# A planned order of steps, replaced: a four-layer graph network whose instruction order is the result of annealing

## The chip, the core and the metric

The kernel runs on one core of a Trainium2 chip. A core has five engines with queues of their own: TensorE (PE, matrix products; PEld is its loading of weights), VectorE (DVE), ScalarE (ACT), GpSimd (POOL) and SyncE (SP), which here only issues transfers. Transfers run on 16 DMA engines that all queues share. The metric is the device time of one execution in microseconds (us); lower is better. The kernel before takes 2910.88 us (median of three runs, 2910.64 to 2910.99).

## The reference

There are 32 graphs (B) of 512 nodes (N) with 256 features (D) each, all in float32. Four layers follow each other; after each there is a residual addition and a normalisation over the features. Cut to what is computed:

```python
def _layernorm(x, axis=-1, eps=1e-5):
    m = jnp.mean(x, axis=axis, keepdims=True)
    v = jnp.var(x, axis=axis, keepdims=True)
    return (x - m) / jnp.sqrt(v + eps)
# layer 0: two-layer perceptron on aggregated neighbours
aggregated = jnp.einsum('bnm,bmd->bnd', adj, x)
h = (1.0 + eps) * x + aggregated
return jax.nn.relu(h @ W1 + b1) @ W2 + b2
# layer 1: four heads, additive scores, edges where adj > 0.5
e = jax.nn.leaky_relu(e_dst[:, :, :, None] + e_src[:, :, None, :], 0.2)
attn = jax.nn.softmax(jnp.where(mask, e, MASK_VAL), axis=-1)
out = jnp.einsum('bhij,bjhf->bihf', attn, h)          # + bias
# layer 2: eight heads, dot products, log of the adjacency added
scores = jnp.einsum('bhqd,bhkd->bhqk', q, k) / math.sqrt(HEAD_DIM)
attn = jax.nn.softmax(scores + jnp.log(adjacency + 1e-06)[:, None, :, :], axis=-1)
out = out.transpose(0, 2, 1, 3).reshape(b, n, HIDDEN) @ Wo.T + bo
# layer 3: scores through one matrix, times adj, nodes masked
similarities = jnp.einsum('bsd,btd->bst', matrix @ W, matrix) * adj
attn = jax.nn.softmax(jnp.where(key_mask, similarities, NEG_INF), axis=-1)
output = jnp.einsum('bst,bth->bsh', attn, matrix)
```

## The kernel before

The work is cut into some 370 small steps per graph, plus 71 that prepare the weights once (`prepare`, line 331, called graph 0). Each graph (`graph`, line 560 on) goes through the four layers, and steps of five to six graphs are in progress at once. A step has a name, an engine, a cost in us written in the code, the steps that it must follow, the buffers that it takes and frees, and for TensorE a mode. The instructions of a step are written out when the planner reaches it; the order in which it reaches them is the order of each engine's queue, since the kernel is recorded under a manual schedule (line 1458). So the order of everything, transfers included, is a product of the class `Plan` (line 47).

`Plan.order` (line 136) is a list scheduler. It keeps a clock for each engine. At each turn it looks at all ready steps of the graphs in its window, finds the earliest start, and takes, of those that can start within `ahead` of it, the one with the smallest due time. The due time of a step is

```python
due = turn[g] * period - self.left[g][name] + moved[name] + stay * change
```

`turn` is the graph's number (moved earlier for the last graphs by `rush`), `left` the longest chain of costs behind the step, `moved` an amount for each step name, and `change` what the planner believes a change of TensorE's mode costs, weighted by `stay`. `moved` is the sum of two things: the list of moves given for each name, and random disturbances that are replayed from seeds:

```python
for seed, far in shifts:
    rng = random.Random(seed)
    for n in moved:
        if rng.random() < 0.15:
            moved[n] += rng.uniform(-far, far)
```

`Plan.run` (line 217) plays each parameter set that it is given, keeps the best, and writes the instructions out; here one set is given. Since `moved` goes by name, every graph is treated alike, and in the middle of the run each graph's steps come in the same order.

The steps that matter below (k is a block of 128 keys of half of the heads, c a block of 128 nodes, the first digit of the names of layers 1 to 3 often the layer or head):

- Layer 0: `h0 h1` (line 728), `f0` to `f3` (751), `y0 y1` (770). `he`, `fe` are their evacuations by ScalarE. `at` (695) transposes the adjacency.
- Layer 1: `xt10 xt11` transpose x (798), `xe10 xe11` evacuate them and sum (802), `v10` to `v13` (819) are the values. `R` is an exponential of the scores; `Rt` transposes it (857), `Rsi` writes it to DRAM (867), `Rli` reads it back to all partitions (874). `z` (922, ScalarE) and `zm` (933, VectorE) make the weights of each head. `o100 o101 o110 o111` (956) multiply them with the values: first digit after o1 the pair of heads, second the half of the nodes. `as` (983, VectorE) adds each head's four blocks up, `d1` (993) sums over the partitions.
- Layer 2: `s0` to `s7` (1115) are four scores at once on 32 rows each, `e` their exponentials (1128, ScalarE), `m` the product with the adjacency (1137, VectorE), `n0` to `n7` (1173) the products with the values. `cd` and `fd` (1148, 1201) are transfers by POOL's queue that add one block of weights onto another, so that `d2` (1220) needs few matmuls. `xt20 xt21 q k v2` come before these, `p0 p1` (1299) after.
- Layer 3: `xt30 xt31`, `i0 i1` (1343), `t0` to `t3` (1357), `ta tb` (1373, 1379), `te` (1387), `u` (1396), `w` (1411).

On TensorE, `s` uses 32 rows of the array, `o1` 64 columns, `n` and `d1` 32 columns, `d2` 64 rows and 32 columns, and all other steps the whole array. The planner knows them as modes `row`, `c64` and `c32`. PSUM has 8 banks; each `s` step takes four of them, which its exponentials free.

Of the kernel before, what the change touches and what calls it, by code (L numbers as in the profile page):

```python
# [227 lines left out]
def fast_path(  # L228
# [71 lines left out]
    def blk(i):  # L300
# [3 lines left out]
    plan = Plan({  # L304
        "B": 11, "C": 12, "D": 18, "p": 8,

        "live": 6, "L0": 1, "L1": 2, "L2": 2, "L3": 1, "AT": 4, "zs": 7, "edge": 1, "tmp": 2,
    })
# [1147 lines left out]
    for g in range(B):  # L1456
        graph(g)
    with tc.manual_schedule():
        plan.run([(24, 0.1, 6, 165.0, ((959604, 5.0), (114893, 5.0), (451585, 5.0), (104136, 2.0), (561761, 2.0), (241046, 2.0), (593942, 2.0), (984585, 2.0)), (2.0, 1.1, 0.1), (('R', 0.5), ('Re', -5.0), ('Rl.q', 20.0), ('Rli', -15.0), ('Rs.q', 3.0), ('Rsi', 6.5), ('Rt', -62.0), ('ST', -37.5), ('ab', 6.0), ('as00', 6.5), ('as01', 6.0), ('as10', 0.5), ('as11', -1.0), ('as20', -27.0), ('as30', -86.5), ('as31', -18.5), ('at0', 3.0), ('at1', 2.0), ('at2', 9.5), ('at3', 6.0), ('atd0', -20.0), ('atd1', 0.5), ('atd2', -30.0), ('atd3', -21.0), ('ate0', 6.5), ('ate1', -13.0), ('ate2', 16.5), ('ate3', 19.0), ('cd1', 29.5), ('cd2', 17.0), ('cd3', 1.0), ('cd5', 39.5), ('cd6', 15.0), ('cd7', 33.5), ('cq1', -4.0), ('cq2', -78.0), ('cq3', 15.0), ('cq5', -20.0), ('cq6', -20.5), ('cq7', 2.0), ('d1', -25.0), ('de', 9.5), ('dev1.0', 27.0), ('dev2.0', 24.5), ('dev3.0', 12.5), ('dev4.0', 55.0), ('dt', 5.5), ('e00', 7.0), ('e01', -4.0), ('e02', 7.0), ('e03', 18.0), ('e10', 3.5), ('e11', 68.5), ('e12', -4.0), ('e13', 7.5), ('e20', 11.0), ('e21', -9.0), ('e22', 3.0), ('e23', -7.5), ('e30', -4.0), ('e31', -8.0), ('e32', 15.0), ('e33', 34.5), ('e40', -1.0), ('e41', -6.5), ('e42', 7.0), ('e43', -41.0), ('e50', 3.0), ('e51', 11.5), ('e52', 30.5), ('e53', 55.5), ('e60', 2.0), ('e61', -31.5), ('e62', 22.0), ('e63', 7.5), ('e70', 5.0), ('e71', 42.0), ('e72', 8.5), ('ed0', 32.0), ('ed1', -5.0), ('ed2', 72.0), ('f0', 19.0), ('f2', -0.5), ('f3', 8.0), ('fd0', 35.5), ('fd1', 41.0), ('fe0', -14.5), ('fe1', -1.0), ('fe2', -8.0), ('fe3', -4.0), ('fq0', -10.5), ('fq1', -10.0), ('h0', 19.0), ('h1', -8.0), ('he0', 2.5), ('he1', -14.0), ('hsb.q', 37.5), ('hsl', 7.0), ('i0', 6.0), ('i1', 7.0), ('ie0', -3.5), ('ie1', -1.0), ('k0', 2.0), ('k1', 18.5), ('ke0', 63.0), ('ke1', 2.0), ('la0.q', -74.0), ('la0i', -35.5), ('la1.q', -166.5), ('la1i', -58.5), ('la2.q', -21.5), ('la2i', 3.0), ('la3.q', -48.0), ('la3i', 4.0), ('lb0.q', -17.5), ('lb0i', -18.5), ('lb1.q', -2.0), ('lb1i', -15.5), ('lb2i', 6.0), ('lb3.q', -40.5), ('lb3i', -20.5), ('ldn.q', -0.5), ('ldni', 3.0), ('lx.q', -17.5), ('lxi', 9.0), ('m00', 2.5), ('m01', 9.0), ('m10', -16.0), ('m11', 12.5), ('m20', 6.5), ('m21', 0.5), ('m30', 4.5), ('m31', -4.5), ('m40', 13.0), ('m41', -31.5), ('m60', -24.0), ('m61', 42.5), ('m70', -1.0), ('m71', 19.5), ('n0', -2.0), ('n1', -31.0), ('n2', -6.5), ('n3', 6.0), ('n4', -3.5), ('n5', -12.0), ('n6', -12.5), ('n7', 32.5), ('nd0', 17.0), ('nd1', 32.0), ('no0', 0.5), ('no1', 9.5), ('node', 27.5), ('o100', 1.0), ('o101', 5.5), ('o110', 6.0), ('o111', 7.0), ('oe0', 23.5), ('oe1', 11.5), ('out0.q', 3.0), ('p0', 35.5), ('p1', 10.5), ('q0', 1.5), ('q1', -87.5), ('qe0', -27.0), ('qe1', -14.0), ('r10', 2.5), ('r11', 7.0), ('r12', 13.0), ('r13', -22.0), ('r20', 87.0), ('r21', 2.0), ('r22', -12.0), ('r23', 10.0), ('r30', 99.5), ('r31', -41.0), ('r33', 24.5), ('r40', -2.0), ('r41', -8.0), ('r42', -66.5), ('r43', 53.5), ('rc00', 5.0), ('rc10', 6.0), ('rc11', 6.5), ('rd1', -21.5), ('rd30', -68.5), ('rd31', 15.0), ('rd32', -5.5), ('rd33', -67.5), ('s0', 4.0), ('s1', -6.5), ('s2', -9.5), ('s3', -41.5), ('s4', -18.5), ('s5', -17.0), ('s6', -18.0), ('s7', -42.0), ('sh1.0', -1.0), ('sh2.0', 92.5), ('sh3.0', 59.0), ('sh4.0', -0.5), ('st10', -13.5), ('st11', 5.0), ('st12', -1.5), ('st13', 40.5), ('st20', -15.5), ('st21', 139.0), ('st22', 13.0), ('st23', 55.5), ('st30', 6.5), ('st31', 36.0), ('st32', 24.0), ('st33', -2.5), ('st40', -22.0), ('st41', 26.0), ('st42', -3.5), ('st43', 96.0), ('t0', 10.5), ('t1', -1.0), ('t2', -14.5), ('t3', -8.5), ('ta0', 27.0), ('ta1', 15.0), ('ta2', -3.5), ('ta3', -2.0), ('tb0', 4.5), ('tb1', -5.5), ('tb2', 4.0), ('tb3', -29.0), ('te0', -17.0), ('te1', -19.5), ('te2', 26.0), ('te3', -3.5), ('u0', -0.5), ('u1', -26.0), ('u2', 6.5), ('u3', 1.0), ('ue0', 17.0), ('ue1', 26.5), ('ue2', 30.5), ('ue3', -1.0), ('v10', 9.5), ('v11', -37.5), ('v12', 2.5), ('v13', -11.5), ('v20', 2.0), ('v21', -1.0), ('v22', -5.0), ('v23', 2.0), ('va1.0', 6.0), ('va2.0', 9.5), ('va3.0', 9.0), ('va4.0', 34.5), ('ve10', -5.5), ('ve11', -25.0), ('ve12', 9.5), ('ve13', -25.5), ('ve20', -1.5), ('ve21', 14.5), ('ve22', -6.0), ('ve23', -6.0), ('w0', 9.0), ('w1', 5.0), ('w2', 9.5), ('w3', -4.0), ('wx0', -29.5), ('wx2', 2.0), ('wx3', 21.5), ('x10', 1.0), ('x11', 1.0), ('x30', 1.0), ('x31', -10.0), ('xd1', -14.5), ('xd2', -5.0), ('xd3', -0.5), ('xe10', 4.0), ('xe11', -0.5), ('xe20', -3.0), ('xe21', -19.0), ('xe30', -23.5), ('xq1', -16.5), ('xq3', -45.0), ('xsi', -6.0), ('xt10', -46.5), ('xt11', -4.0), ('xt20', -6.0), ('xt30', -6.5), ('xt31', -5.5), ('y0', 9.5), ('y1', -4.0), ('yd00', -12.0), ('yd01', 59.5), ('yd10', 11.5), ('yd11', 88.0), ('yn0', -131.5), ('yn1', 9.0), ('yn2', -131.5), ('yn3', 17.5), ('yt0', 9.0), ('yt1', -21.5), ('yt2', -16.0), ('yt3', -18.0), ('z00', 13.5), ('z02', 104.5), ('z03', -3.0), ('z10', -4.5), ('z11', 12.0), ('z12', 3.0), ('z13', -2.0), ('z20', 22.0), ('z22', -11.5), ('z23', -6.5), ('z30', -2.0), ('z31', -39.0), ('z32', 21.5), ('z33', -7.0), ('zm00', -27.5), ('zm01', 56.5), ('zm10', -8.0), ('zm11', 21.5), ('zm20', 8.5), ('zm21', 0.5), ('zm30', 3.0), ('zm31', 28.5)))])

# [427 lines left out]
@with_exitstack  # L1890
def four_layer_graph_kernel(ctx: ExitStack, tc: tile.TileContext, *args):
    flags = ctx.enter_context(tc.tile_pool(name="flags", bufs=1))
    beyond = flags.tile([1, 1], I32, name="beyond")
    fast_path(tc, *args, beyond)
    taken = tc.nc.values_load(beyond, min_val=0, max_val=1,
                              skip_runtime_bounds_check_because="is_lt gives 0 or 1")
    with tc.If(taken > 0):
        general_path(tc, *args)
# [34 lines left out]
```

## Time and profile before

| what | value |
|---|---|
| median of the runs | 2910.88 us |
| the profiled execution, whole | 2910.6 us |
| its span, first to last instruction | 2908.8 us |
| instructions in the profile | 42662 |
| granted TensorE clock, mean | 0.998 |
| VectorE, ScalarE, POOL busy | 2256.4, 1903.9, 454.9 us |
| transfers | 430.70 MB, 148 GB/s on average |
| TensorE's idle time by its waits, longest single ones | 4.9 us (adjacency), 4.5 us (x), 2.1 us (L956 for L1028) |

The profile is of one execution, so sums are made against its own span, and the 1.8 us between the span and the whole are kept apart. A group of instructions shows its busy time and the mean length of one; a window shows the busy time of each engine in a stretch; the chain of waits follows the end of the program back, piece by piece. The profile's matmul lengths run past the start of the next matmul, since they overlap; the distance from one start to the next is what a matmul costs.

### The profile page before, as it was taken

What the parts mean: (1) busy time and instruction counts of PE and PEld (TensorE: products, weight loads), DVE (VectorE), ACT (ScalarE), POOL (GpSimd) and SP (SyncE); (2) the same over time, 40 slices, a digit from 0 to 9 for tenths busy, and PEclk for the clock granted to TensorE, in tenths of its full rate; (3) what the DMA queues carried; (4) which work ended last, traced back from release to release, by engine and by line L of the source; (5) the groups of instructions that cost most, each with busy time, mean ns of one, the idle gap of its engine ahead of it and who ended that gap; (6) DMA issues with size and microseconds to landing.
All of it is one profiled execution on the core that took longest, in us unless ns stands there. A gap on an engine that the chain in (4) does not pass through costs nothing.

```text
span 2908.8 us, 42662 instructions
## 1 busy us (share of the span) xinstructions
PE 2878.8 (99%) x15521; PEld 1655.2 (57%) x15521; DVE 2256.4 (78%) x4389; ACT 1903.9 (65%) x3818; POOL 454.9 (16%) x494
## 2 busy tenths in 40 slices
PE   8989999999999999999999999999999999999998
PEld 6645555556555566555565555665555655556445
DVE  2786788777888777887778887778877788887975
ACT  3676666776656766667766567666667665676754
POOL 1111111111111111111111111111111111111110
PEclk9999999999999999999999999999999999999999
DMA  6367775567866567765678665677656786665851
GB/s 186 70 153 150 159 170 135 137 145 167 186 142 139 134 160 174 165 141 137 140 165 187 145 138 134 159 172 165 145 138 137 163 187 147 138 144 126 183 120 41
DMA packets 134879, 430.70 MB, mean 148 GB/s; under 512 B 13628, under 2 KB 53384, under 8 KB 102792
## 3 DMA queue, kind: packets, MB, share of 16 engines
q0 software_dynamic: 45568, 277.89, 49.2%
q1 hardware_dynamic: 88112, 149.75, 15.4%
q8 instruction: 125, 2.05, 0.3%
q14 instruction: 90, 0.74, 0.1%
q10 hardware_dynamic: 984, 0.28, 0.1%
HBM read 183.25 MB, written 17.08 MB: 69 GB/s over the span
## 4 chain that ended last, share of the span: by engine, by line
PE 95%; DMA 2%; ACT 1%; DVE 1%; issue 0%; POOL 0%; POOLq 0%; ACTq 0%; SPq 0%
PE s L1115 9%; PE o_ps L1173 8%; PE hT_ps L728 8%; PE o_ps L1411 8%; PE s L1357 8%; PE y_ps L770 8%; PE o_ps L956 7%; PE h1T_ps L751 7%; PE iT_ps L1343 4%; PE v_ps L819 4%; PE o2p_ps L1299 4%; PE kT_ps L1078 4%; PE qT_ps L1078 4%; PE v_ps L1096 4%; PE xT_t L1059 2%; PE eT_t L1396 2%
## 5 line engine op out<-in xcount | busy, mean ns | idle before, releaser
L1128 ACT ACTIVATE z<-s 128x512 f32<-128x512 f32 x1024 | 558.9, 609 | 131.4 <-PE s L1115 101.6
L1137 DVE SCALAR_TENSOR_TENSOR z<-AT,z 128x1024 f32<-128x1024 f32 x512 | 603.0, 1207 | 36.4 <-ACT z L1128 36.0
L933 DVE SCALAR_TENSOR_TENSOR z<-z,T,edge 128x512 f32<-128x512 f32 x512 | 363.7, 747 | 157.7 <-ACT z L922 156.9
L922 ACT ACTIVATE z<-R_bc,nT,S 128x512 f32<-128x512 f32 x512 | 395.5, 819 | 8.4 <-PE y_ps L770 3.0
L641 ACT ACTIVATE x<-x,shift,rstd 128x256 f32<-128x256 f32 x508 | 296.1, 609 | 152.0 <-DVE shift L631 152.0
L1148 POOL DMA_DIRECT2D z<-z x186 | 166.8, 903 | 1029.4 <-DVE nmax L1379 254.5
L623 POOL TENSOR_TENSOR rstd<-ve,nhalf 128x4 f32<-128x4 f32 (+1 forms) x131 | 153.5, 1172 | 978.2 <-DVE ve L617 953.8
L1115 PE MATMUL s<-qT,kT 32*128 32x512 f32 x2048 | 287.4, 633 | 1.0 <-ACT kT L1084 1.0
L1173 PE MATMUL o_ps<-z,v 128*32 128x512 f32 x2048 | 267.4, 602 | 1.8 <-DVE z L1137 1.7
L956 PE MATMUL o_ps<-z,v 128*64 128x512 f32 x1024 | 240.5, 601 | 2.1 <-DVE y L1028 2.1
L983 DVE TENSOR_TENSOR z<-z 128x1024 f32<-128x1024 f32 (+1 forms) x256 | 231.4, 952 | 13.0 <-PE o_ps L956 12.9
L1411 PE MATMUL o_ps<-x,eT 128*128 128x256 f32 x1024 | 239.3, 382 | 0.7 <-ACT eT L1401 0.7
L751 PE MATMUL h1T_ps<-hT,w_sb 128*128 128x512 f32 x512 | 230.4, 593 | 0.0
L1357 PE MATMUL s<-xT,iT 128*128 128x512 f32 x512 | 226.6, 594 | 0.7 <-ACT z L1128 0.7
L770 PE MATMUL y_ps<-w_sb,h1T 128*128 128x256 f32 x1024 | 226.7, 379 | 0.0
L1263 DVE RECIPROCAL rdT<-rdT 128x256 f32<-128x256 f32 x128 | 219.1, 1731 | 2.1 <-ACT rdT L1256 2.0
L600 DVE BATCH_NORM_STATS2 st<-x 128x6 f32<-128x256 f32 x508 | 211.0, 415 | 7.5
L1411 PEld LDWEIGHTS o_ps<-x,eT 128*128 128x128 f32 x1024 | 187.5, 190 | 46.3 <-ACT z L1387 21.0
L728 PE MATMUL hT_ps<-AT,x 128*128 128x384 f32 (+2 forms) x768 | 210.2, 383 | 0.0
L770 PEld LDWEIGHTS y_ps<-w_sb,h1T 128*128 128x128 f32 x1024 | 194.1, 190 | 27.9 <-issue 0.8
L1115 PEld LDWEIGHTS s<-qT,kT 32*128 32x128 f32 x2048 | 86.0, 183 | 166.0 <-ACT z L1128 118.8
L825 ACT COPY v<-v_ps 128x264 f32<-128x264 f32 x128 | 47.9, 376 | 183.7 <-PE v_ps L819 183.2
(155 smaller groups left out, 4241.3 us busy)
## 6 DMA issues: line engine op xcount, KB each, us to landing
z<-z POOLq DMA_DIRECT2D x186, 1024.0 KB, 8.5
A<-in_adj_dram SPq DMA_DIRECT2D x256, 256.0 KB
x<-biases POOLq DMA_DIRECT2D x96, 512.0 KB, 7.1
R_bc<-R_dram SPq DMA_DIRECT2D x32, 1024.0 KB
z<-z POOLq DMA_DIRECT2D x62, 512.0 KB, 8.7
x<-in_x_dram SPq DMA_DIRECT2D x32, 512.0 KB
out_dram<-x SPq DMA_DIRECT2D x31, 512.0 KB
nm<-in_nodemask_dram SPq DMA_DIRECT2D x32, 256.0 KB
```

The lines of the kernel that those rows point to most:

```text
L728: nc.tensor.matmul(ph[:, cols], t["x"][:, m, blk(d)], moving, start=(k == 0), stop=(k == len(parts) - 1),)
L751: nc.tensor.matmul(ph, w1_sb[:, d, blk(f)], t["hT"][:, d, :], start=(d == 0), stop=(d == DC - 1))
L770: nc.tensor.matmul(py[:, j, :], t["h1T"][:, f, blk(2 * c2 + j)], w2_sb[:, f, :], start=(f == 0), stop=(f == HC - 1),)
L922: nc.scalar.activation(t[f"e{h}"][:, c, :], t["Rbc"][:, h, :], AF.Relu, bias=t["nT"][:, h, c : c + 1], scale=t["S"][:, h, c : c + 1],)
L933: nc.vector.scalar_tensor_tensor(z, z, t["T"][:, h, c : c + 1], t["edge"][:, c, :], op0=ALU.add, op1=ALU.mult)
L956: nc.tensor.matmul(po[j * F1 : (j + 1) * F1, :], t["v"][:, c, h * F1 : (h + 1) * F1], t[f"e{h}"][:, c, :], start=(c == 0), stop=(c == NC - 1),
L1115: nc.tensor.matmul(pk, t["k"][hs, o, blk(c)], t["q"][hs, o, :], start=True, stop=True)
L1128: nc.scalar.activation(t[f"E{k}"][:, j, :], t[f"ps{k}{j}"], AF.Exp, scale=QSCALE)
L1137: nc.vector.scalar_tensor_tensor(z, t["AT"][:, c, None, :].to_broadcast([P, 2, N]), ADJ_EPS, z, op0=ALU.add, op1=ALU.mult,)
L1173: nc.tensor.matmul(t[f"n{o}"][32 * j : 32 * j + 32, :], t["v2"][:, c, o * P + F2 * j : o * P + F2 * (j + 1)], t[f"E{k}"][:, j, :], start=( ...
L1357: nc.tensor.matmul(pt, t["iT"][:, d, blk(c)], t["xT3"][:, d, :], start=(d == 0), stop=(d == DC - 1),)
L1411: nc.tensor.matmul(py, t[f"eT{c}"][:, blk(m)], t["x"][:, m, :], start=(m == 0), stop=(m == NC - 1),)
```

## The change

One line changes, the parameter set of `plan.run` in line 1459. The period (24), `ahead` (0.1) and the window (6 graphs) stay. `stay` goes from 165 to 80. The list of seeds grows from 8 to 14, with reaches of 2.0 and 5.0. `rush` goes from (2.0, 1.1, 0.1) to (1.7, 1.0, 0.0). The list of moves is new throughout: 317 names instead of 323. No instruction, buffer size or cost changes. The core of the diff, with the one long line wrapped:

```diff
-        plan.run([(24, 0.1, 6, 165.0,
-            ((959604, 5.0), (114893, 5.0), (451585, 5.0), (104136, 2.0),
-             (561761, 2.0), (241046, 2.0), (593942, 2.0), (984585, 2.0)),
-            (2.0, 1.1, 0.1),
...
-            ('Rt', -62.0), ('d1', -25.0), ('i1', 7.0), ('n0', -2.0), ('n1', -31.0), ('n3', 6.0),
-            ('o110', 6.0), ('o111', 7.0), ('s0', 4.0), ('t0', 10.5), ('t1', -1.0), ('xt31', -5.5)
...
+        plan.run([(24, 0.1, 6, 80.0,
+            ((959604, 5.0), (114893, 5.0), (428442, 5.0), (827982, 2.0), (379309, 5.0),
+             (168251, 5.0), (904211, 5.0), (197558, 5.0), (201498, 2.0), (728276, 2.0),
+             (358280, 2.0), (281265, 2.0), (22270, 2.0), (235352, 2.0)),
+            (1.7, 1.0, 0.0),
...
+            ('Rt', -85.5), ('d1', -79.5), ('d2', -2.0), ('i1', -29.0), ('n0', 19.0), ('n1', 8.0),
+            ('n3', 12.5), ('o110', 26.0), ('o111', 2.5), ('s0', 2.5), ('t0', 9.5), ('t1', -3.0),
+            ('xt31', -31.0)
...
```

What comes of it is an order. TensorE's steps of one period in the middle, from one graph's `h0` to the next one's (the steps belong to six graphs), before:

```
h0 h1 p1 n7 xt20 xt21 f0 f1 f2 k0 q0 q1 f3 k1 v20 v21 v22 y0 y1 xt30 xt31 v23
s0 s1 o100 o101 s2 n0 d2 o110 n1 s3 o111 d1 s4 i0 s5 n2 s6 i1 s7 n3
xt10 xt11 t0 t1 t2 t3 dt v10 v11 v12 v13 yt0 yt1 yt2 yt3 u0 n4 n5 n6
w0 u1 p0 Rt u2 u3 w1 at0 at1 at2 at3 w2 w3
```

and after:

```
h0 h1 w3 p1 n7 xt20 xt21 f0 f1 f2 k0 f3 q0 v20 v21 v22 k1 v23 q1 y0 y1 xt30 xt31
s0 s1 o100 o101 s2 d2 n0 o110 o111 s3 n1 d1 s4 i0 i1 s5 n2 s6 t0 s7 t1
xt10 xt11 t2 v10 v11 v12 t3 v13 dt yt0 yt1 yt2 n3 n4 n5 n6 yt3
u0 u1 p0 u2 w0 Rt u3 at0 at1 at2 at3 w1 w2
```

VectorE's steps around `s0` to `d1`, before and after:

```
m00 as10 m01 m10 as11 as00 m11 as01 as30 as20 as31 as21
m00 sh1.0 m10 as00 m01 as01 as10 m11 as11 as30 as20 as31 as21
```

On ScalarE `z10` follows `he1` directly; before, three normalising steps of an earlier graph (`r40` to `r42`) stood around `he1`, ahead of `z10`. On SP the reading back of `R` (`Rli`) moves from the end of a period into the start of the next one.

## The prediction

> **What bounds the kernel now.** I read the page first: engine shares, then the waits of TensorE, the windows, the chain of waits in order of time, and last the timeline of one period.
>
> ```profile
> PE 2878.8 (99%) x15521; PEld 1655.2 (57%) x15521; DVE 2256.4 (78%) x4389; ACT 1903.9 (65%) x3818; POOL 454.9 (16%) x494
> ```
>
> TensorE is busy for 99%, no other engine over 78%. "Busy" hides how much of it is forced, so the windows (span, then busy time of PE, PEld, DVE, ACT, POOL, clock, DMA share, GB/s) split it:
>
> ```profile
> 140.00:240.00 100.00, 91.31 (x535) 42.44 (x533) 85.55 (x149) 70.16 (x138) 15.79 (x16) 0.98 0.61 136
> 417.00:2546.70 2129.70, 2129.70 (x11562) 1227.55 (x11561) 1687.17 (x3261) 1419.81 (x2856) 338.18 (x360) 1.00 0.67 153
> ```
>
> From 417 to 2547 us TensorE never idles. Its visible idle time is in the fill, worst between 140 and 240 us, and a little in the drain. The chain of waits shows the middle to be periodic:
>
> ```profile
> 1012.22 6.87 PE s L1357 x16
> ...
> 1101.03 6.87 PE s L1357 x16
> ```
>
> The same piece returns after 88.81 us, and does so for every graph in the middle. So the time is fill + about 24 equal periods + drain, and a period is as long as TensorE's own instructions. What an order can change there is what TensorE pays between unlike steps. The timeline of one period (start, length, instruction) prices it; I take start to next start, not the printed lengths:
>
> ```profile
> 1024.00 2.78 PE L1173 MATMUL o_ps<-z,v 128*32 128x512 f32 x24
> 1026.71 1.99 PE L1411 MATMUL o_ps<-x,eT 128*128 128x256 f32 x8
> ...
> 1076.35 3.65 PE L956 MATMUL o_ps<-z,v 128*64 128x512 f32 x16
> 1079.93 1.14 PE L1115 MATMUL s<-qT,kT 32*128 32x512 f32 x8
> 1081.00 1.07 PE L1173 MATMUL o_ps<-z,v 128*32 128x512 f32 x8
> 1082.00 1.09 PE L1220 MATMUL d_ps<-z,ones 64*32 64x512 f32 x16
> 1083.02 1.94 PE L956 MATMUL o_ps<-z,v 128*64 128x512 f32 x8
> 1084.88 1.06 PE L1173 MATMUL o_ps<-z,v 128*32 128x512 f32 x8
> 1085.88 1.14 PE L1115 MATMUL s<-qT,kT 32*128 32x512 f32 x8
> 1086.95 1.94 PE L956 MATMUL o_ps<-z,v 128*64 128x512 f32 x8
> 1088.82 1.08 PE L993 MATMUL d_ps<-z,pick 128*32 128x128 f32 x32
> 1089.83 1.14 PE L1115 MATMUL s<-qT,kT 32*128 32x512 f32 x8
> 1090.90 1.98 PE L1343 MATMUL iT_ps<-xT,w_sb 128*128 128x512 f32 x4
> 1092.82 1.14 PE L1115 MATMUL s<-qT,kT 32*128 32x512 f32 x8
> ```
>
> Each column of shapes names a tiling of the array: 32*128 (s), 128*64 (o1), 128*32 (n, d1), 64*32 (d2), 128*128 (all else). **Price of a change of tiling:** two o1 steps together take 1079.93-1076.35 = 3.58, one alone 1.86 or 1.87, so the second costs 1.72 and closing a stretch 0.15. Three n together take 2.71, one alone 1.00: each further n 0.86, closing 0.14. By the same subtraction (1.93 for two s just ahead of this stretch, 1.07 for one) a stretch of s costs 0.21. Four L1343 matmuls between two s take 1.92, while inside a full-array stretch they follow each other at 0.43, 1.72 in all: entering and leaving full-array work costs 0.20. n directly followed by d2 takes 1083.02-1081.00 = 2.02 = 1.00+1.02: those two, of different tilings, save nothing.
>
> **What the Trainium skill says.** "TensorEngine Tiling (Array Packing)", Key Properties: changing the tiling mode, not just the tile, drains TensorE. The trace agrees and gives the size, 0.14 to 0.21 us, and shows that n to d2 counts as a change. "Perfetto Trace Analysis", Tensor Engine Instruction: a matmul's end is an estimate, and ScalarE and VectorE run strictly in order; hence start to start above, and queue sums below. The trace agrees: the printed lengths overlap the next start by 0.07. "DMA: Bandwidth & Descriptors", Queues, rings and completion order: each DMA engine takes its queues in turn, packet by packet, so a small transfer waits behind large ones. The trace agrees: the 8 KB write of R is issued at 1031.63, while three of POOL's adds of 0.5 to 1 MB are in flight, and the read that waits for it goes out at 1040.24.
>
> **The change, part by part.** No instruction is added or removed on TensorE; both programs hold the same 8827 matmuls. I compared the two instruction orders. From graph 7 both repeat one period of 74 TensorE steps.
>
> 1. *Merges in the period.* o110 now runs directly before o111 (n1 and s3 were between): -0.15. n1 runs directly before d1, both 128*32: -0.14. n3 moves from behind s7 to the group n4 n5 n6: -0.14. Stretches of s stay at seven, of full-array work at five. Sum -0.43: the period becomes 88.38.
> 2. *d2 before n0 instead of after.* n to d2 saves nothing; d2 to n is not in the trace. Bound: 0 to -0.14 a period; I take 0.
> 3. *i1 now directly behind i0, t0 alone between s6 and s7.* Full-array stretches stay five: 0.
> 4. *Whole program.* Cut wherever the tiling changes, the order has 726 stretches before, 650 after: full-array 183 to 180, s 225 to 226, o1 94 to 71, and of 32-column work 257 to 204 pieces (d2 its own piece). 3x0.20 + 23x0.15 + 53x0.14 - 0.21 = **-11.2 us**; about 24x0.43 = 10.3 of it lies in the periods. All of it is on TensorE, which is the path, so nothing hides it, unless a wait takes its place.
> 5. *The wait at d1.* This is the one I expect to appear. d1 needs the eight additions `as`. In the old trace they end the VectorE burst
>
> ```profile
> 1078.33 1.23 DVE L983 TENSOR_TENSOR z<-z 128x1024 f32<-128x1024 f32 x1 [0.35 <-PE o_ps L956]
> ...
> 1084.62 4.16 DVE L983 TENSOR_TENSOR z<-z 128x512 f32<-128x512 f32 x5
> ```
>
> without a gap: 11 operations from 1078.33 to 1088.78, and d1 starts at 1088.82, 0.04 later and just not delayed. The new order holds the same three L1137 and eight L983, but starts with m10, which waits for the fifth exponential after s0. These come every 0.485 from 1075.63, so the fifth ends near 1078.18; the burst then ends at 1078.20+10.45 = 1088.65. TensorE comes to d1 sooner: up to 1081.00 as before, d2 n0 to 1083.02, o110 o111 +3.58 = 1086.60, s3 +1.07 = 1087.67, n1 +0.86 = 1088.53. d1 reads the last sum in its third matmul, so it waits about 1088.69-1088.54 = 0.15. Queued behind d1 are s4, i0, i1 and all of TensorE; nothing hides it. Bound 0 to 0.20; I take 0.15, 24 times: **+3.6**. If d2 to n0 saves 0.14 after all, d1 waits that much longer: this burst sets the period.
> 6. *Other tight places.* The new order puts v10 1.7 us behind the second transpose xt11 (7.0 before); the evacuation needs about 0.1 + 0.6 + 0.2 for its read of the sum and a hop, and the one ahead of it may push it by 0.3: 1.2, so no wait. s1 follows xt31 by one s step, 0.95; its bank is free after 0.83: no wait, 0.1 at most. SP: R's broadcast now falls into the next period; see rival D. POOL: the adds of E7 and fd0, and the reciprocal roots, swap places by one; the first user is tens of us later.
> 7. *Fill.* From the first transpose (4.93) to graph 7's first h step (416.94) is 412.0; its matmuls, at the prices above, come to 381.2: 30.8 are lost. VectorE is busy for 85.55 of 100 us there, so it can't shrink much. Graph 5's h0 stood behind n2 of graph 2, which needs 149.9 us of VectorE work in queue order; now it stands behind n1, which needs 146.9. That is a gain of up to 3; I take **-2**, bounds -6 and +9 (one POOL add took 17.4 us to land at 188 and held ScalarE, 8.9 over the median 8.5). The drain loses 5.1 now; its order looks alike, 0 +-2.
>
> Sum on the profiled execution: span 2908.8 - 11.2 + 3.6 - 2.0 = 2899.2; 1.8 lies around it (2910.6): 2901.0. The median of the runs stands 0.28 above that execution: **2901.3**.
>
> **The rivals.** *A*, the forecast: 2901.3, own range 2897 to 2905. For it: the middle has no jitter, the same period returns to 0.01 us.
> *B*: no wait at d1, fill gains 4: 2910.9-11.2-4 = 2895.7. For: as21's end beats my sum if ScalarE's fifth exponential is early. Against: the burst had 0.04 to spare.
> *C*: the fill eats the gain: half of one late add on the chain, 2910.9-11.2+3.6+4.5 = 2907.8. For: it happened at 188 us. Against: the order of the adds there is nearly the old one.
> *D*, slower: R's row. Its transpose Rt stood 7.8 us before the next h0, now 5.65, and its first user z10 is reached 7.7 after h0 instead of 9.6. z10 never waited, so the broadcast landed within 8.0 us of its issue at h0+1.6; 2.1 later that is by h0+11.7. z10 heads ScalarE's queue for xe20, xe21, then k0 at h0+17.6; it costs nothing until it starts later than h0+15.0. If the write sticks behind more adds and the broadcast takes the 10.5 us that one piece of the chain in the fill shows, it lands near h0+16.3, 1.3 late, 24 times: 2901.3+31 = 2932. Against: it needs 3.3 us more than the upper bound.
> *E*: the merges pay less than their price, as n to d2 does: 2910.9.
>
> **How the numbers follow.** A 0.50, B 0.22, C 0.16, D 0.08, E 0.04. 0.2% is 5.8 us, about what a measurement can tell from no change; below 2905.1 lie nearly all of A, B and a quarter of C: faster 0.73; most of C, E and the rim of A: same 0.19; D: slower 0.08. The range 2894 to 2909 takes in A, B and C with the bounds of d1 and of the fill.
>
> **What would show it.** A period near 88.5 in the chain; 88.38 exactly speaks for B, 88.81 for E, over 89 for D with ScalarE waiting at L922 for the broadcast. o1 twice together at 3.58, n+d1 at 1.87, four n at 3.57. A wait of 0.15 at L993 for L983 in every period. h0 of graph 7 near 413. I am wrong if a wait outside d1 repeats in every period: 0.25 there undoes 6 of the 9.6 us.

## The result, and the profile after

| | before | after |
|---|---|---|
| median of the runs | 2910.93 us (2910.64 to 2913.06, 4 runs) | 3034.01 us (3020.70 to 3042.33, 4 runs) |
| ratio after/before, 95% interval | | 1.0417 [1.0372, 1.0462] |
| the profiled execution, its span | 2910.6, 2908.8 us | 3041.18, 3039.4 us |
| first h step of graph 7 (end of the fill) | 416.9 us | 421.7 us |
| from there to graph 31's (24 periods) | 2129.7 us | 2247.8 us |
| from there to the end (the drain) | 362.2 us | 370.0 us |

The change makes the kernel 4.2% slower. The forecast was 2901.3, with 0.73 on faster, so it failed on the sign as well as on the size. Of the 130.6 us between the two spans, 118.1 lie in the middle, 4.7 in the fill and 7.8 in the drain.

The page after: engine shares, the chain of waits by engine and by line, and one group of ScalarE.

```profile
PE 2920.2 (96%) x15521; PEld 1684.0 (55%) x15521; DVE 2240.0 (74%) x4389; ACT 1921.6 (63%) x3818; POOL 453.3 (15%) x494
...
PE 72%; DMA 19%; ACT 5%; DVE 2%; issue 1%; SPq 0%; POOL 0%; ACTq 0%; POOLq 0%; DVEq 0%
...
L922 ACT ACTIVATE z<-R_bc,nT,S 128x512 f32<-128x512 f32 x512 | 403.0, 818 | 257.9 <-DMA R_bc<-R_dram 253.9
```

TensorE is down from 99% to 96%, and transfers are 19% of the chain. The same group of ScalarE before:

```profile
L922 ACT ACTIVATE z<-R_bc,nT,S 128x512 f32<-128x512 f32 x512 | 395.5, 819 | 8.4 <-PE y_ps L770 3.0
```

There `z` (L922) lost 8.4 us in all; now 253.9 us end with the arrival of R's broadcast. The windows say where TensorE idles (span, busy time of PE, PEld, DVE, ACT, POOL, clock, DMA share, GB/s). The first is the middle, the second a short stretch behind one of its waits:

```profile
422.00:2669.00 2247.00, 2166.89 (x11557) 1256.04 (x11556) 1669.68 (x3258) 1437.21 (x2856) 338.63 (x360) 0.98 0.64 145
...
537.60:544.40 6.80, 5.50 (x7) 2.40 (x8) 4.54 (x14) 6.80 (x13) 1.09 (x1) 0.50 0.58 121
```

The middle, which had no idle microsecond, now has 80. TensorE's waits (total, times, longest):

```profile
PE kT_ps L1078 <- ACT xT L1063: 77.4, 20, 7.0
PE AT_t L695 <- DMA A<-in_adj_dram: 12.3, 2, 7.4
PE xT_t L1059 <- ACT x L641: 8.2, 18, 2.3
```

The first comes once in most periods: `k0` waits for the evacuation `xe20`, which stands behind `z10` in ScalarE's queue. The second is in the first 14 us, and 5.4 us of the third are in the fill too. The chain of waits in one of the slow periods names what `z10` waits for (start, length, piece):

```profile
511.47 0.12 PE R_t L857
...
512.23 13.47 DMA R_dram<-R_rows
...
525.71 11.05 DMA R_bc<-R_dram
...
538.38 0.48 ACT xT L1063
...
538.90 3.78 PE kT_ps L1078 x4
542.68 2.65 PE h1T_ps L751 x4
```

From `Rt` to `k0` 27.4 us pass, and 24.5 of them are two transfers: R's 8 KB row written to DRAM (13.47) and read back to all partitions (11.05; the read fills every partition, 1 MB in all). Each period begins with `h0`; from one `h0` to the next it took 88.81 every time before. After, between graphs 7 and 30, 4 periods of 23 take 88.56 to 88.76 and the others 91.2 to 98.0. So the order itself is faster, by 0.25 a period, and something that varies is laid on top.

The waits are not the whole loss. Without slow periods the new order's middle takes 2123.7 us (loads_behind_all, below); here it takes 124.1 more, 80.1 of them idle and 44.0 in which TensorE is busy for longer with the same matmuls. The clock records of the trace show why: in this middle the granted clock stands at half for 16 stretches of 3.41 or 6.83 us, 95.6 us together, and in the middle of the kernel before and of loads_behind_all for none. 15 of the 16 begin 2.1 to 5.4 us after a wait of `k0` began. The window from 537.60 above is one. The chain shows its price, the two groups of four matmuls behind the wait, which take 3.78 and 2.65; in the kernel before `k0` and a group of the same L751 took

```profile
1054.67 1.72 PE kT_ps L1078 x4
...
1059.82 1.72 PE h1T_ps L751 x4
```

So the 80.1 us of waits come with about half as much again behind them.

### The profile page after: what moved, and what is told of

It reads as the page before. It is cut to its first block, busy times and chain, and to the rows that moved or that the text cites. A ratio compares the mean times of both kernels' runs of the same rounds, so it can differ in the third digit from the quotient of the medians.

```text
span 3039.4 us, 42699 instructions
## 1 busy us (share of the span) xinstructions
PE 2920.2 (96%) x15521; PEld 1684.0 (55%) x15521; DVE 2240.0 (74%) x4389; ACT 1921.6 (63%) x3818; POOL 453.3 (15%) x494
## 4 chain that ended last, share of the span: by engine, by line
PE 72%; DMA 19%; ACT 5%; DVE 2%; issue 1%; SPq 0%; POOL 0%; ACTq 0%; POOLq 0%; DVEq 0%
DMA R_dram<-R_rows 9%; PE s L1115 8%; PE s L1357 7%; PE o_ps L1173 7%; PE o_ps L956 7%; DMA R_bc<-R_dram 6%; PE y_ps L770 6%; PE kT_ps L1078 4%; PE iT_ps L1343 4%; PE v_ps L819 4%; PE h1T_ps L751 3%; PE o_ps L1411 3%; PE qT_ps L1078 3%; PE v_ps L1096 3%; ACT z L922 3%; PE hT_ps L728 3%
## 5 line engine op out<-in xcount | busy, mean ns | idle before, releaser
L1128 ACT ACTIVATE z<-s 128x512 f32<-128x512 f32 x1024 | 539.9, 610 | 98.6 <-PE s L1115 93.0
L922 ACT ACTIVATE z<-R_bc,nT,S 128x512 f32<-128x512 f32 x512 | 403.0, 818 | 257.9 <-DMA R_bc<-R_dram 253.9
L641 ACT ACTIVATE x<-x,shift,rstd 128x256 f32<-128x256 f32 x508 | 290.0, 615 | 151.7 <-DVE shift L631 151.5
L1148 POOL DMA_DIRECT2D z<-z x186 | 164.4, 885 | 1078.7 <-PE s L1115 308.7
L1173 PE MATMUL o_ps<-z,v 128*32 128x512 f32 x2048 | 258.8, 602 | 2.0 <-DVE z L1137 1.9
L1357 PE MATMUL s<-xT,iT 128*128 128x512 f32 x512 | 244.4, 605 | 0.0
L751 PE MATMUL h1T_ps<-hT,w_sb 128*128 128x512 f32 x512 | 240.1, 613 | 1.9 <-ACT hT L735 1.9
L983 DVE TENSOR_TENSOR z<-z 128x512 f32<-128x512 f32 (+1 forms) x256 | 231.1, 952 | 4.4 <-PE o_ps L956 4.3
L1078 PE MATMUL kT_ps<-xT,wkT 128*128 128x512 f32 x256 | 149.5, 714 | 77.4 <-ACT xT L1063 77.4
L899 DVE CUSTOM_DVE_ANT_0 xs_row<-xs_row,wgT 128x256 f32<-128x256 f32 x64 | 27.2, 425 | 218.5 <-DMA xs_row<-xs_dram 217.4
```

The source lines that it names most:

```text
L751: nc.tensor.matmul(ph, w1_sb[:, d, blk(f)], t["hT"][:, d, :], start=(d == 0), stop=(d == DC - 1))
L922: nc.scalar.activation(t[f"e{h}"][:, c, :], t["Rbc"][:, h, :], AF.Relu, bias=t["nT"][:, h, c : c + 1], scale=t["S"][:, h, c : c + 1],)
L1078: nc.tensor.matmul(pq, wT[n][:, d, blk(o)], t["xT2"][:, d, :], start=(d == 0), stop=(d == DC - 1))
L1128: nc.scalar.activation(t[f"E{k}"][:, j, :], t[f"ps{k}{j}"], AF.Exp, scale=QSCALE)
L1173: nc.tensor.matmul(t[f"n{o}"][32 * j : 32 * j + 32, :], t["v2"][:, c, o * P + F2 * j : o * P + F2 * (j + 1)], t[f"E{k}"][:, j, :], start=( ...
L1357: nc.tensor.matmul(pt, t["iT"][:, d, blk(c)], t["xT3"][:, d, :], start=(d == 0), stop=(d == DC - 1),)
```

## Where the row of R loses its time

Median times of the middle periods, from the instruction and packet records of the trace; h0 is the next graph's first h step, the loads are the four of A3 (L1327, the adjacency for layer 3, 1 MB together):

```
                              before   after
R's write issued               -7.0    -4.8   relative to h0
loads, issue to last packet     8.3    20.7
R's write, issue to last packet 7.1    11.8
write's issue to read's issue   8.05   12.95
read's issue to z10             8.0    10.7
z10 starts                     +9.1   +19.0   relative to h0
```

Of the 9.9 us that `z10` is later, 2.2 are the later transpose, which the prediction had counted, 4.9 are the write and 2.7 the read. SP's queue shows the setting. First a period before, then one after (start, length of the issue, line):

```profile
1021.00 3.46 SPq L1327 DMA_DIRECT2D A<-in_adj_dram  x4
1031.32 0.25 SPq L884 DMA_DIRECT2D xs_dram<-R_rows  x1
1031.63 1.49 SPq L867 DMA_DIRECT2D R_dram<-R_rows  x1
1040.24 0.34 SPq L874 DMA_DIRECT2D R_bc<-R_dram  x1
```

```profile
503.29 3.33 SPq L1327 DMA_DIRECT2D A<-in_adj_dram  x4
511.92 0.25 SPq L884 DMA_DIRECT2D xs_dram<-R_rows  x1
512.23 0.33 SPq L867 DMA_DIRECT2D R_dram<-R_rows  x1
525.71 0.34 SPq L874 DMA_DIRECT2D R_bc<-R_dram  x1
```

Relative to the next h0 (1038.62 and 517.05) the loads are issued 17.6 us ahead before and 13.8 ahead after. Their place follows `t3`: SP waits with the load of x (L677) for the buffer that `t3` (L1357) frees, and the change puts `t3` 3.6 us later, behind `t2 v10 v11 v12`. In the period before, the loads' packets run from 1023.6 to 1029.5 and are mostly gone when POOL's adds (L1148, 8 KB packets) come at 1027.1. After, they run from 506.4 to 524.7, beside adds from 509.1 on, and the row's packets, issued at 512.23 on the same queue, go out at 521.3 to 525.0, with the last of the loads. That the adds are what slows the loads is read from this coincidence; no run took the adds away.

Three theories follow. *The ring*: the row stands in SP's own queue (its ring) behind loads that crawl, that is, take 20.7 us instead of 8.3. *Lateness*: the 2.2 us of the later transpose are the cause, and everything after them bunches. *The engines*: the adds take the 16 DMA engines, whatever queue the row is on.

## The experiments

Edits of the order are made on the planner's result: a named step of graph g is moved to right ahead of or behind a named step of graph g+n, for g from 8 to 28 where nothing else is said, so that the graphs ahead of these keep the old order within the same run. Medians in us; the kernel before, run beside each group, gave 2911.3 to 2912.0. The last column is of one execution each, the profiled one. Its middle repeats well (2121.5 or 2121.6 in four runs that share it), its fill and drain do not: five runs with the same start give fills of 413.6 to 418.3.

| run | median | ratio to before, 95% interval | middle (24 periods), fill, drain |
|---|---|---|---|
| loads_behind | 2941.4 | 1.0096 [1.0079, 1.0113] | 2146.5, 422.0, 372.8 |
| Rt_early | 3031.0 | 1.0393 [1.0368, 1.0418] | 2239.5, 423.2, 381.4 |
| R_on_act_queue | 2920.3 | 1.0028 [1.0019, 1.0038] | 2126.8, 421.0, 371.6 |
| old_loads_ahead | 3069.6 | 1.0532 [1.0511, 1.0552] | 2274.5, 418.5, 373.8 |
| act_queue_e11 | 2917.7 | 1.0022 [1.0014, 1.0029] | 2124.0, 418.0, 371.6 |
| old_two_merges | 2911.7 | 1.0002 [0.9993, 1.0010] | 2130.7, 416.8, 362.1 |
| loads_behind_all | 2912.3 | 0.9999 [0.9991, 1.0007] | 2123.7, 414.9, 374.9 |
| all_repairs | 2911.6 | 0.9999 [0.9990, 1.0008] | 2121.6, 416.0, 369.7 |
| drain_cd2 | 2918.5 | 1.0022 [1.0012, 1.0031] | 2121.6, 418.3, 374.2 |
| drain_cd2_lb | 2914.6 | 1.0013 [1.0006, 1.0020] | 2121.5, 416.0, 371.3 |
| repairs_lb | 2908.7 | 0.9989 [0.9982, 0.9995] | 2121.5, 413.6, 366.5 |

### 1. The loads behind the row

```diff
 SP, in every period of the changed kernel
-nm  A3_0 A3_1 A3_2 A3_3  xs  R_dram  R_bc  xs_row
+nm  xs  R_dram  R_bc  xs_row  A3_0 A3_1 A3_2 A3_3
```

Here `nm` is the node mask, `xs` a row of 1 KB that leaves with R's row, and `xs_row` its reading back.

> The changed kernel, but on SP's queue the four loads of A3 (L1327) stand behind the broadcast of R (L874) instead of ahead of its write (L867), in the periods of graphs 11 to 31; nothing else moves. Theory 1, the ring (R's 8 KB write waits in SP's own ring behind loads that crawl): the write lands in 3 to 5 us instead of 13 to 14.5, z10 starts before h0+15.5, the periods are 88.56 and the time is about 2900 (2895 to 2910). Theory 2, lateness (the transpose Rt stands 2.1 us later): the write is issued as late as before, z10 stays late, no change, 3020 to 3040. Theory 3, the engines (POOL's adds of 0.5 to 1 MB take the DMA engines): the adds are as they were, the write takes 8 us or more, some periods stay slow, 2950 to 3010.

2941.4, above the range that the ring theory gave. The trace says why: graphs 7 to 9 and 11 still have periods of 94.4, 95.4, 96.5 and 90.5, and from graph 12 on 17 of 18 take 88.56 (one 88.88). The edits begin with graph 8's loads, and these stood ahead of graph 11's row, which graph 12's period is the first to need; so the slow periods end where the edit begins. The row's last packet now comes 5.8 us after its issue instead of 11.8, `z10` starts at +9.7 instead of +19.0. The transpose is as late as in the changed kernel and the adds are as they were. This speaks against lateness, and for the ring.

### 2. The transpose early

```diff
 TensorE, in the changed kernel (and ST, R on ScalarE, Re on VectorE)
-w0 Rt u3
+Rt w0 u3
```

> The changed kernel, but ST, R and the transpose Rt stand ahead of w0 instead of behind the stretch of w steps, and VectorE's copy Re of R's row ahead of yn3, so that the write of R (L867) is issued about 1.7 us sooner; the loads stay where they are. Theory 1, the ring: the write is still queued behind the same loads and lands when they land, so z10 gains 0 to 0.5 us and the time is 3015 to 3040. Theory 2, lateness: everything behind it comes 1.7 us sooner, some 18 slow periods gain up to 1.7 each, 2995 to 3012. Theory 3, the engines: the write meets the adds 1.7 us sooner, gain below 1 a period, 3010 to 3040.

3031.0: no gain beyond the runs' spread (3017 to 3046). The row's write is issued 1.7 us sooner (-6.5 instead of -4.8), takes 14.4 instead of 12.95 until the read can be issued, and so the read goes out only 0.4 us sooner, at +7.9. It waits for the loads and not for its own issue. Lateness is refuted as the cause.

### 3. The row on another queue

```diff
-            nc.sync.dma_start(t["Rdram"], t["Rr"][: H1 * NC, :])
+            nc.scalar.dma_start(t["Rdram"], t["Rr"][: H1 * NC, :])
```

> The changed kernel, but the write of R (L867) is issued by ScalarE on its own DMA queue instead of by SP; the loads, the adds and the broadcast (L874, still SP) stay. Theory 1, the ring: the write no longer stands behind the loads and lands in 3 to 6 us instead of 13 to 14.5; the broadcast that follows on SP's ring still stands behind what is left of the loads, so z10 gains 3 to 8 us a slow period and the time is 2900 to 2980. Theory 2, lateness: the write is issued no sooner, 3020 to 3045. Theory 3, the engines: the write shares the same 16 engines with the adds on any queue and takes 10 us or more, 3015 to 3045.

2920.3, inside the ring's range. Order, loads and adds are those of the changed kernel; in the trace the loads crawl as there (20.0 us from issue to last packet, 20.7 there), and still the row's last packet comes 4.3 us after its issue. ScalarE issues it, and SP can read back 5.5 us later instead of 12.95:

```profile
505.40 0.31 ACTq L867 DMA_DIRECT2D R_dram<-R_rows  x1
```

```profile
504.43 0.26 SPq L884 DMA_DIRECT2D xs_dram<-R_rows  x1
510.87 0.33 SPq L874 DMA_DIRECT2D R_bc<-R_dram  x1
517.75 0.32 SPq L891 DMA_DIRECT2D xs_row<-xs_dram  x1
```

The small write of `xs` (1 KB, L884), still on SP's queue behind the loads, shows the rest: its reader L891 is issued 13.3 us after it here (median 11.3; 8.0 in loads_behind_all). 20 of 23 periods take 88.56, three 88.94 to 90.14. So the share of the engines that adds and loads take isn't what holds the row; its place behind the loads in SP's queue is. The Trainium skill, "DMA: Bandwidth & Descriptors", Queues, rings and completion order, has SP and ACT own separate rings; this pair of runs agrees, 4.3 us against 11.8. The read, on SP's queue, takes 10.8 us until `z10`, as in the changed kernel (10.7), beside the rest of the loads: here `z10` is at +12.2, when the loads are behind it is at +9.7.

### 4. The old kernel with its loads late

```diff
 SP, in every period of the kernel before
-nm  A3_0 A3_1 A3_2 A3_3  xs  R_dram  R_bc  xs_row
+nm  xs  A3_0 A3_1 A3_2 A3_3  R_dram  R_bc  xs_row
```

> The kernel before, but the four loads of A3 (L1327) are moved on SP's queue from their place some 17 us before the next h0 to right ahead of the write of R (L867), so that they come about 7 us before h0; Rt, the adds and all else stay. Theory 1, the ring: the write now stands behind 1 MB of loads that run beside the adds, lands 8 us or more later, z10 starts beyond h0+15.5 in most periods, and the kernel before becomes slow: 2960 to 3060. Theory 2, lateness: Rt is where it was, so at most 0.5 us a period, 2910 to 2922. Theory 3, the engines: the adds are where they were, the loads add some traffic, 2910 to 2940.

3069.6: the old order becomes slower than the changed one, with `Rt` where it was. Up to graph 11 the periods are 88.81; from graph 12 on they take 94.1 to 98.2. But the way isn't the one expected:

```profile
1048.67 0.25 SPq L884 DMA_DIRECT2D xs_dram<-R_rows  x1
1048.97 5.96 SPq L1327 DMA_DIRECT2D A<-in_adj_dram  x4
1054.98 1.34 SPq L867 DMA_DIRECT2D R_dram<-R_rows  x1
1063.05 0.33 SPq L874 DMA_DIRECT2D R_bc<-R_dram  x1
```

SP spends 5.96 us on issuing the four loads (3.46 in the period of the kernel before that is shown above), so the row is issued 6.1 us later; from its issue to its last packet it takes 6.8 us, no more than the 7.1 of the kernel before. The read takes 9.9 us until `z10` instead of 8.0. The run shows that loads ahead of the row on SP cost whole periods, here through SP's time to issue them. It isn't a second proof of the wait in the ring.

### 5. The wait at d1

```diff
 ScalarE, in R_on_act_queue
-e00 e01 e10 e02 e11 e03
+e00 e01 e10 e11 e02 e03
```

> The changed kernel with R's write (L867) on ScalarE's DMA queue (2920.3 us alone), and besides that ScalarE's exponential e11 ahead of e02 instead of behind it, in graphs 8 to 28: e11 ends some 0.48 us sooner, VectorE's burst, which starts with m10, may start when m00 is done (0.25 sooner as the trace shows it), and d1 no longer waits. If the 0.18 us between the period of 88.56 and the ledger's 88.38 is the wait at d1: the period becomes 88.38 to 88.42 and the time falls by 3 to 4.5, to 2916 to 2918. If the 0.18 is instead an error of the merges' prices, the period stays 88.56 and the time 2919 to 2921.

2917.7 and a period of 88.46: the fall is 0.10 a period and not 0.18. First the changed order without slow periods (loads_behind), then this run, TensorE's d1 and s4:

```profile
1559.14 1.24 PE L993 MATMUL d_ps<-z,pick 128*32 128x128 f32 x32
1560.31 1.14 PE L1115 MATMUL s<-qT,kT 32*128 32x512 f32 x8
```

```profile
1531.40 1.13 PE L993 MATMUL d_ps<-z,pick 128*32 128x128 f32 x32
1532.46 1.14 PE L1115 MATMUL s<-qT,kT 32*128 32x512 f32 x8
```

d1, start to next start, takes 1560.31-1559.14 = 1.17 and 1532.46-1531.40 = 1.06; before the change it took 1.01. So 0.16 us of wait were in the changed period, inside d1, and 0.05 are left here. The wait doesn't show as idle time ahead of d1, since only its later matmuls need the last sum.

```diff
 TensorE, in the kernel before
-s2 n0 d2 o110 n1 s3 o111 d1 s4
+s2 n0 d2 o110 o111 s3 n1 d1 s4
```

> The kernel before with only two of the merges, in graphs 8 to 28: o111 right behind o110, and n1 right ahead of d1 (order o110 o111 s3 n1 d1). Loads, R's row and VectorE's order stay. The prices say -0.29 a period. If d1 is tied to VectorE's burst, as the prediction has it, d1 can come at most 0.16 sooner (it starts 0.04 behind the end of the last sum now, and 0.12 ahead of it where it waits): period 88.65 to 88.75, time 2907 to 2910. If nothing ties d1: period 88.52, time about 2905. If the merges do not pay at all: 2911.

2911.7, period 88.81 (one of 23 takes 89.47): no gain at all, outside the range that was given for a tied d1. The timeline shows a gain and its return:

```profile
1527.58 3.65 PE L956 MATMUL o_ps<-z,v 128*64 128x512 f32 x16
1531.16 1.14 PE L1115 MATMUL s<-qT,kT 32*128 32x512 f32 x8
1532.23 1.06 PE L1173 MATMUL o_ps<-z,v 128*32 128x512 f32 x8
1533.11 1.34 PE L993 MATMUL d_ps<-z,pick 128*32 128x128 f32 x32
1534.39 1.14 PE L1115 MATMUL s<-qT,kT 32*128 32x512 f32 x8
```

o110 and o111 take 3.58 together and n1 0.88 ahead of d1, 0.27 less than apart; d1 takes 1.28 instead of 1.01, 0.27 more. In this kernel, the one before, loads_behind and act_queue_e11 alike, s4 starts 1.05 after the end of VectorE's last sum (1533.34 here). So VectorE's burst, which in the old order starts from `o100`, sets this point of the period already in the kernel before, and a merge between `o100` and `d1` pays only as far as the burst is shortened too.

### 6. The fill, and what is left

```diff
 SP
 A3 loads behind the row as in 1, for graphs 1 to 28
-A_0 x w_sb w_sb wg_sb A_1 A_2 A_3 rawq        (start, graph 1)
+A_0 A_1 A_2 A_3 x w_sb w_sb wg_sb rawq
```

> The changed kernel with two edits of SP's queue: the loads of A3 behind R's broadcast for graphs 1 to 28 (8 to 28 in the first run of this kind, 2941.4 us), and at the very start the last three strips of graph 1's A ahead of x and the weights, as in the kernel before. If the four slow periods that were left (20.7 us over 88.56 in all) came from loads that the first run had not moved, they go: -21. If the 5 us that the fill lost came from the strips that were issued at 9.8 us instead of 1 to 2, they go too: -5. Together 2913 to 2919; without the second 2918 to 2923; if the slow periods have another cause, 2935 or more.

2912.3: both effects go, 0.7 below the range. All 23 periods are 88.56, the fill ends at 414.9, and only the drain (374.9) stands against the order. The changed kernel's start had SP issue three of the first graph's four strips after x and the weights:

```profile
0.76 0.40 SPq L670 DMA_DIRECT2D A<-in_adj_dram  x1
1.21 0.42 SPq L677 DMA_DIRECT2D x<-in_x_dram  x1
...
8.69 1.29 SPq L670 DMA_DIRECT2D A<-in_adj_dram  x3
```

The run makes both edits, but the strips can be told apart from the loads: graph 2's first h step, ahead of any A3 load that was moved, comes at 35.1 to 38.7 us in the five runs with the strips first, and at 41.6 to 44.9 in the five runs of the changed order without them.

All four repairs together:

> The changed kernel with all repairs: loads of A3 behind R's broadcast, strips of graph 1 first, R's write on ScalarE's queue, e11 ahead of e02. Fill as in the kernel before or 2 us more (417 to 419 us up to graph 7's first h step), 24 periods at 88.38 to 88.42, drain between the old 362 and the 371.6 that the kernel with R's write on ScalarE's queue shows: 2900 to 2912. Below 2909 it beats both kernels; if the drain stays at 371 or more it ties with the kernel before at 2908 to 2912.

2911.6 (2903.5 to 2919.4), inside the range, on the side where the drain eats the gain: 2121.6 us in the middle against 2129.7 before, 369.7 in the drain against 362.2. The period is 88.46, above the 88.38 to 88.42 expected, and the fill 416.0, below its 417 to 419. The chain through the worst of the drain there:

```profile
2705.35 21.42 DMA z<-z
...
2743.83 1.76 PE d_ps L1220 x14
```

Three adds of graph 30 start within 2 us, beside the 1 MB of loads of A3 of graph 29, and the last takes 21.4 us; in the kernel before the same three start over 12 us, beside the same loads, and take 9.2 to 15.8. Two edits of this place:

```diff
 POOL, adds of graph 30 (xd3 is a transfer of graph 31)
-cd5 cd2 cd7 cd6 xd3 fd0 fd1
+cd5 cd7 cd6 cd2 xd3 fd0 fd1
```

> All repairs (2911.6 us), and besides that, in graph 30 alone, POOL's add cd2 behind cd6 instead of between cd5 and cd7. In the drain three adds of 1 MB are in flight together beside the loads of A3 there, the last of them takes 21 us, and the chain of waits runs through it, cd6 and fd1 to d2. If three adds at once are what stretches the chain: cd5 and cd7 share the engines between two, land 5 us sooner, and the time falls by 3 to 5 us to about 2907; d2's order of adds then ends with fd0. If the bytes in flight, and not their order, set the end (cd2 and fd0 still have to land before d2): 0 to -1, 2910.5 to 2912.

2918.5: slower by about 7 us, where both views gave no loss; the profiled drain is 4.5 longer. The add cd7 took 15.0 instead of 21.4 us, as meant, but cd2 is issued 18 us later and the transfer of biases behind it (L587) takes 13.3 instead of 10.1; TensorE now stands idle for 6.6 us at a v2 step (L1096) of graph 31 instead of 1.8 at a d2 step (L1220). The stall moved to another step.

```diff
 SP, besides the edit above
-(graph 29) A3_0 A3_1 A3_2 A3_3 ... out (graph 28)
+(graph 28) out ... A3_0 A3_1 A3_2 A3_3 (graph 29)
```

> The same, and the four loads of A3 of graph 29 (1 MB, issued beside those adds) behind the output write of graph 28, some 38 us later; VectorE needs them 32 us after that. If the loads share the engines with the chain's adds: another 2 to 4 us, 2903 to 2907. If the adds alone set it: no more than drain_cd2 gives, within 1 us.

2914.6 and a drain of 371.3 instead of 374.2: the time misses its range, while the gain on drain_cd2, 3.9 us in the medians and 2.9 in the one drain of each, is inside the 2 to 4 given for it. So the later place of the loads was kept, for graphs 28 and 29, and POOL's edit dropped:

> All repairs (2911.6 us), POOL's order as there, and the loads of A3 of graphs 28 and 29 behind the output writes of graphs 27 and 28 instead of behind R's broadcast: they then start some 25 and 38 us later, beside fewer of the drain's adds. The pair of drain kernels showed 2.9 us of the drain for graph 29's loads alone. If bytes in flight set the drain: its length falls from 369.7 to 365 to 368 and the time to 2906 to 2910, which would beat the kernel before by up to 0.2%. If the adds alone do: 2911 to 2913.

2908.7, drain 366.5, both inside their ranges: 0.11% faster than the kernel before (0.05 to 0.18%), the lowest median here. The profiled execution is a fast one of this kernel, 2903.4, so its drain flatters, and that the loads made the step from all_repairs (2.9 us, with single times that overlap from 2903.5 to 2913.7) isn't shown. At the median, fill and drain together take 2908.7 - 1.8 - 2121.5 = 785.4 us, 6.3 more than the 779.1 before. That part stays open: the new order has POOL's adds closer together in the drain, and it wasn't tried to spread them without delaying another.

## Why the prediction was wrong

The forecast's sum is 140.2 us short of the profiled execution: 124.8 in the middle, 6.7 in the fill, 7.8 in the drain, and 0.9 are the merges foretold outside the middle.

- *Steps 1 to 4, the merges*: right. o1 twice takes 3.58 and the four n 3.57 as foretold, n1 ahead of d1 0.88 (0.86); d2 then n0 take 2.02, as n then d2 did. With only 0.05 of wait left the period is 88.46, so the ledger's 88.38 is 0.03 off. (The sum of step 4 as it is written comes to 11.3, not 11.2.)
- *Step 5, the wait at d1*: right, in its mechanism too. 0.15 forecast, 0.16 measured; periods of 88.53 and 88.56. old_two_merges and act_queue_e11 show that it is VectorE's burst. Only the 0.04 us that the old burst was said to have to spare was none.
- *Step 6, the other tight places*: here it failed. The step put R's broadcast off to rival D, and D's bound is the false one: "z10 never waited, so the broadcast landed within 8.0 us of its issue at h0+1.6; 2.1 later that is by h0+11.7". It took the queue and the lengths of both transfers as fixed and added only the shift of the transpose. But the same change had moved six other transfers of SP's queue, through `t3` and the wait of L677, so that the loads of A3 among them ran into the adds. The write takes 4.9 us longer, the read 2.7, and `z10` starts at +19.0. The price of D, 1.3 us a period and 2932, was the bound's edge: the mean is 93.66 a period against 88.49 in loads_behind_all, 5.2. D priced the lateness alone and one for one; of the 5.2, 3.3 are idle time and 1.8 the half clock behind it. D's place, `z10` ahead of `k0`, holds, and so does its word that the write sticks, though in SP's own queue behind loads and not behind the adds; its point of decision nearly holds: with `z10` at +13.9 k0 keeps its place at +17.6 and the period is 88.76, with `z10` at +16.5 k0 comes at +18.5 and the period is 91.2 (h0+15.0 forecast). It had a chance of 0.08.
- *The reading of the transfer queues*: that they take turns, packet by packet, was read as if a small transfer then waits behind the large ones of other queues. That step was the prediction's own, and R_on_act_queue speaks against it: beside the same adds and loads, but on a queue without loads ahead, the row took 4.3 us.
- What would have told: the timeline of SP shows L1327 between L677 and L867, the waits of SP show 1093.8 us of L677 for L1357, the two orders show `t3` three steps later, and the text itself had noted that the 8 KB write took 8.6 us beside adds. The steps were asked where each waits, the transfers only where their own engine puts them.
- *Step 7, the fill*: wrong by its omission, +4.7 against -2 with a bound of +9. The queue of VectorE was compared, the first dozen issues of SP weren't. With the strips first and the loads behind, it ends at 413.6, 414.9, 416.0, 416.0 and 418.3 in five runs, against 416.8, 416.9 and 418.5 in three with the old order. From graph 2's first h step on, where the start no longer counts, it takes 377.2 to 379.6 us in the five and 378.6 to 379.3 in the three: the gain of 2 isn't shown.
- *The drain, 0 +-2*: wrong, +7.8; "its order looks alike" was a look at TensorE's steps, while POOL's adds stand closer together. That they are the cause is likely from the chain through them, but no edit has undone it.

## What to carry to other kernels

When an order changes, list for each small transfer on the path what stands ahead of it in its own queue, and when those loads now run: a load that is moved into a burst of large transfers can keep its queue shut for what follows. Price a wait of TensorE with the clock that the trace grants behind it, not with its own length alone. A bound taken from a wait that never occurred holds only while everything that shares the queue stays where it is. A step that lets itself be shortened gains nothing as long as another engine's burst sets the point behind it; that burst's end, measured against the next step's start, tells so before the edit.

## What was not expected of the hardware

- 1 MB in loads with 2 KB packets took 8.3 us from issue to last packet where most of it went out ahead of POOL's adds, and 20.7 us beside the adds with their 8 KB packets (medians). In old_loads_ahead, issued later still, it took 13.0.
- An 8 KB write behind the crawling loads on their queue took 11.8 us to its last packet; on ScalarE's queue, beside the same loads and adds, 4.3 us.
- Issuing four such loads held SP for a median of 3.5 us in the kernel before and of 6.3 us (3.4 to 7.4) in old_loads_ahead, where POOL's adds were in flight; in the changed kernel, where they were issued ahead of the adds' packets, it was 3.1.
- TensorE's granted clock fell to half for 3.41 or 6.83 us at 15 of 19 waits of `k0` in the middle of the changed kernel, the shortest of them 2.35 us long; the four without were of 0.76 to 3.04 us.
